# A group's row sums copied ahead of its product with the targets, and waiting for the gathers

## The chip, the cores and the metric

The kernel runs on one core of one Trainium2 chip. The metric is device time of one execution in microseconds (us), the median of three runs. Five engines work side by side, each through its own instruction stream in order: TensorE (PE in the profile, its weight loads PEld), VectorE (DVE), ScalarE (ACT), GpSimd (POOL) and SyncE (SP). They wait for each other through semaphores: an instruction waits until a counter has reached a value, and adds to a counter when it is done. An instruction carries one wait here; further ones stand ahead of it on the same engine as instructions of their own (EVENT_SEMAPHORE in the profile).

## What is computed

For 16,384 users, each with 100 items of history and one target, out of a table of 50,001 items:

```
def _neighbor_attn(E, near_full):
    V = E[near_full]                                  # 32 neighbours of each item
    scores = einsum('nd,nkd->nk', E, V) / sqrt(32)
    return einsum('nk,nkd->nd', softmax(scores), V)
a_sus, a_inf = _neighbor_attn(E_in, near_full), _neighbor_attn(E_out, near_full)
h = concat([E_hist[history], a_sus[history], a_inf[history]])   # 16384 x 100 x 128
t = concat([E_tgt[target],   a_inf[target],  a_sus[target]])    # 16384 x 128
z = relu(einsum('bld,hd->blh', h * t[:, None, :], W1) + b1)     # 128 hidden
scores = einsum('blh,h->bl', z, W2[0])
exp_A = exp(scores) * ((history != target[:, None]) & (history != 0))
attn = exp_A / sum(exp_A, -1)[:, None] ** 0.5
s = sum(h * attn[..., None])                                    # one number
pred = cosine(s * ones, t);   return sigmoid(pred)
```

Of `h * attn` only the sum over everything is wanted, so the kernel needs of each history row its 128 values for the product with the target, and the sum of those values.

## The kernel before, in words

Everything is float32. There are two stages and a short end.

**Stage one** computes the neighbour attention of all items and writes two tables to device memory. `table` holds per item a row of 129 numbers (`W`): first the sum of the item's 128 values, then the values. `ttab` holds the target's values. The change does not touch this stage.

**Stage two** goes through the users in chunks of 128 (`UC` = 128 chunks, one user per partition), and through a chunk's 100 history items in groups of four (`LG`; `NG` = 25 groups a chunk), so through 3200 steps `s`. All engines run it in an order written out by hand. A step issues, in this order:

- `gather(s)`, line 309: four indirect DMAs on POOL (line 316), each of which fetches one row of `table` for each of the 128 users into a buffer `h` of 128 x 4 x 129. There are 20 such buffers (`HBUF`), so the gathers of step s+20 go to the buffer of step s, and wait until all that reads it is done.
- `turn(s)`, line 326: four PE transposes (line 330) turn the 128 values of the four rows into `hT_ps`, one of three PSUM buffers.
- `times_target(s)`, line 332: DVE multiplies `hT_ps` by the chunk's target `tT` into `xT` (line 335, one of six buffers), and then copies the four row sums of `h` to `hsum` (line 338). That copy reads `h` in SBUF itself. It is declared free of a dependency on the four gathers, with the reason that TensorE has read the row: the product before it on DVE waits for the transposes, and these wait for the gathers.
- `hidden(s-3)`, line 345: a PE product with W1 into `z_ps` (line 347), and relu on ACT into `z` (line 349).
- `scored(s-6)`, line 351: a PE product with W2 that adds up in `bank` (line 355).

Once a chunk come the gather of the next chunk's targets (line 280) and `target_work` (lines 288 to 307), and `weights`, `exponents` and `ended`, which turn the chunk's scores into its two sums with `hsum` (lines 359 to 380).

So a buffer `h` has two readers: the transposes on PE and the copy on DVE. The first of the four gathers of step s+20 stands behind a separate wait, for its DMA lane and for DVE's counter, and itself waits for PE's counter.

Of the kernel before, what the change touches and what calls it, by code (L numbers as in the profile page):

```python
# [44 lines left out]
NG = L // LG  # L45
# [8 lines left out]
def kernel(  # L54
# [13 lines left out]
    nc = tc.nc  # L68
# [8 lines left out]
    table = dram.tile([ROWS, W], F32, name="table")  # L77
# [40 lines left out]
    def history_of(i):  # L118
        hists[i] = u_in.tile([P, BSUB, L], I32, name="hidx")
        nc.sync.dma_start(hists[i], hist_v[i])  # L120

    with (
# [23 lines left out]
        def gather(b):  # L146
            v = n_v.tile([P, M, K, 2, G], F32, name="v")
            subs[b]["v"] = v
            for m, s in enumerate(subs[b]["tiles"]):
                it, j = divmod(s, NSUB)  # L150
                if j == NSUB // 2 and it + 1 < NITER:
                    load(it + 1)
                nidx = its[it][0]
                for k in range(K):
                    nc.gpsimd.indirect_dma_start(  # L155
                        out=v[:, m, k].rearrange("p t d -> p (t d)"),
                        out_offset=None,
                        in_=egeo,
                        in_offset=bass.IndirectOffsetOnAxis(ap=nidx[:, j, k : k + 1], axis=0),
                    )  # L160
# [105 lines left out]
    with (  # L266
        tc.manual_schedule(engines={E.PE, E.Activation, E.DVE, E.SP, E.Pool}),
        tc.tile_pool(name="u_x", bufs=6) as u_x,
        tc.tile_pool(name="u_z", bufs=6) as u_z,
        tc.tile_pool(name="u_s", bufs=3) as u_s,  # L270
        tc.tile_pool(name="ps_t", bufs=3, space=bass.MemoryType.PSUM) as ps_t,
        tc.tile_pool(name="ps_z", bufs=3, space=bass.MemoryType.PSUM) as ps_z,
        tc.tile_pool(name="ps_s", bufs=2, space=bass.MemoryType.PSUM) as ps_s,
    ):
        users = {}
        rows, got, hT, xT, z = {}, {}, {}, {}, {}

        def target_rows(c):
            t = u_t.tile([P, D], F32, name="t")
            nc.gpsimd.indirect_dma_start(  # L280
                out=t,
                out_offset=None,
                in_=ttab[0:ITEMS, :],
                in_offset=bass.IndirectOffsetOnAxis(ap=tidx[:, c : c + 1], axis=0),
            )
            users[c] = {"t": t, "hidx": hists[c // BSUB][:, c % BSUB, :]}

        def target_work(c):
            u = users[c]
            t = u["t"]  # L290
            tT_ps = ps_t.tile([P, LG, P], F32, name="hT_ps")
            nc.tensor.transpose(tT_ps[:, 0, :], t, ident)  # L292
            tT = u_t.tile([D, 1, P], F32, name="tT")
            nc.vector.tensor_copy(tT[:, 0, :], tT_ps[:, 0, :])  # L294
            u["tT"] = tT
            nc.vector.tensor_reduce(tsum[:, c : c + 1], t, AX.X, ALU.add)
            junk = u_t.tile([P, D], F32, name="junk")
            nc.scalar.activation(junk, t, AF.Square, accum_out=tsq[:, c : c + 1])
            keep = u_s.tile([P, L], F32, name="keep")
            idf = u_s.tile([P, L], F32, name="idf")  # L300
            nc.vector.tensor_copy(idf, u["hidx"])
            nc.vector.tensor_scalar(keep, idf, 0.0, None, ALU.not_equal)
            nc.vector.scalar_tensor_tensor(  # L303
                keep, idf, tidf[:, c : c + 1], keep, ALU.not_equal, ALU.mult
            )
            u["keep"] = keep
            u["hsum"] = u_s.tile([P, L], F32, name="hsum")

        def gather(s):
            c, g = divmod(s, NG)  # L310
            rows[s] = u_h.tile([P, LG, W], F32, name="h")
            got[s] = []
            for q in range(LG):
                l = g * LG + q
                got[s].append(
                    nc.gpsimd.indirect_dma_start(  # L316
                        out=rows[s][:, q, :],
                        out_offset=None,
                        in_=table,
                        in_offset=bass.IndirectOffsetOnAxis(  # L320
                            ap=users[c]["hidx"][:, l : l + 1], axis=0
                        ),
                    )
                )

        def turn(s):
            c, g = divmod(s, NG)
            hT[s] = ps_t.tile([P, LG, P], F32, name="hT_ps")
            for q in range(LG):
                nc.tensor.transpose(hT[s][:, q, :], rows[s][:, q, 1:W], ident)  # L330

        def times_target(s):
            c, g = divmod(s, NG)
            xT[s] = u_x.tile([D, LG, P], F32, name="xT")
            nc.vector.tensor_tensor(  # L335
                xT[s], hT.pop(s), users[c]["tT"].to_broadcast([D, LG, P]), ALU.mult
            )
            copy = nc.vector.tensor_copy(  # L338
                users[c]["hsum"][:, g * LG : (g + 1) * LG],
                rows.pop(s)[:, :, 0:1].rearrange("p q o -> p (q o)"),  # L340
            )
            for one in got.pop(s):
                tc.declare_no_dep(copy.ins, one.ins, reason="TensorE has read the row")

        def hidden(s):
            z_ps = ps_z.tile([HID, LG, P], F32, name="z_ps")
            nc.tensor.matmul(z_ps, w1T, xT.pop(s), start=True, stop=True)  # L347
            z[s] = u_z.tile([HID, LG, P], F32, name="z")
            nc.scalar.activation(z[s], z_ps, AF.Relu, bias=b1_sb)  # L349

        def scored(s):
            c, g = divmod(s, NG)
            if g == 0:
                users[c]["bank"] = ps_s.tile([NG, LG, P], F32, name="bank")
            nc.tensor.matmul(  # L355
                users[c]["bank"], pick[:, g, :], z.pop(s), start=g == 0, stop=g == NG - 1
            )

        def weights(c):
            flat = u_t.tile([NG, LG, P], F32, name="flat")  # L360
            nc.scalar.copy(flat, users[c].pop("bank"))  # L361
            users[c]["flat"] = flat

        def exponents(c):
            flat = users[c].pop("flat")
            score = ps_t.tile([P, LG, P], F32, name="hT_ps")
            for q in range(LG):
                nc.tensor.transpose(score[:, q, 0:NG], flat[:, q, :], ident[0:NG, 0:NG])  # L368
            users[c]["ea"] = u_s.tile([P, L], F32, name="ea")
            nc.scalar.activation(  # L370
                users[c]["ea"].rearrange("p (g q) -> p q g", q=LG), score[:, :, 0:NG], AF.Exp
            )

        def ended(c):
            u = users.pop(c)
            ea = u["ea"]
            nc.vector.tensor_tensor(ea, ea, u["keep"], ALU.mult)
            nc.vector.tensor_reduce(den[:, c : c + 1], ea, AX.X, ALU.add)
            nc.vector.tensor_tensor(ea, ea, u["hsum"], ALU.mult)
            nc.vector.tensor_reduce(num[:, c : c + 1], ea, AX.X, ALU.add)  # L380

        last = UC * NG
        target_rows(0)
        target_work(0)
        for s in range(last + 2 * LAG + 6):
            c, g = divmod(s, NG)
            if s < last:
                if g == 0 and c % BSUB == 2 and 0 < c // BSUB and c // BSUB + 1 < UC // BSUB:
                    history_of(c // BSUB + 1)
                if g == 5 and c + 1 < UC:  # L390
                    target_rows(c + 1)
                gather(s)
                turn(s)
                times_target(s)
            if 0 <= s - LAG < last:
                hidden(s - LAG)
            if 0 <= s - 2 * LAG < last:
                scored(s - 2 * LAG)
            if s < last and g == 15 and c + 1 < UC:
                target_work(c + 1)  # L400
            done, left = divmod(s - 2 * LAG - NG, NG)
            if 0 <= done < UC and left == 0:
                weights(done)
            if 0 <= done < UC and left == 1:
                exponents(done)
            if 0 <= done < UC and left == 4:
                ended(done)
# [79 lines left out]
```

## Time and profile before

| | us |
|---|---|
| median of 3 runs | 36167.52 |
| lowest, highest | 36134.86, 36170.64 |
| profiled execution | 36233.66 |
| its span, first to last instruction | 36231.5 |

| engine | busy us | share of the span |
|---|---|---|
| PE | 9993.2 | 28% |
| DVE | 6913.8 | 19% |
| ACT | 2690.8 | 7% |
| POOL | 25673.9 | 71% |

A line of the profile names the line of the kernel, the engine, the operation, what it writes and reads, how often, then its busy time in us and the mean of one in ns, and after the bar the idle time of its engine just before it and what ended most of that. PE's ends are modelled. A wait that ends with "issue" has no releaser that the profile shows; "remote" is a semaphore event that it cannot put down to an instruction. A queue with a q behind the engine's name (DVEq, POOLq) is what the engine's instruction stream does by itself, such as separate waits. [...]

### The profile page before, as it was taken

Reading aid. Unit: us, or ns where it says so; the run is one execution under the profiler, and the core shown is the slowest. Engines: PE = TensorE matmul, PEld = TensorE weight load, DVE = VectorE, ACT = ScalarE, POOL = GpSimd, SP = SyncE. Lnnn points to the kernel's source line nnn. Section 1 sums busy time; section 2 is a strip of 40 time slices with the busy share of each in tenths; the row PEclk is TensorE's granted clock in tenths of the full one; section 3 lists DMA queues with packets and bytes.
Section 4 is the critical chain, followed back from the end, with each engine's and each line's share of the span. In section 5 each row is a group of like instructions: output and inputs, shape, how many; then the busy total and the mean of one; then the engine's idle time right before and its main releaser. Section 6 shows DMA issues by size and latency. Waiting matters only on the chain.

```text
span 36231.5 us, 104145 instructions
## 1 busy us (share of the span) xinstructions
PE 9993.2 (28%) x26243; PEld 3238.5 (9%) x26243; DVE 6913.8 (19%) x9965; ACT 2690.8 (7%) x5698; POOL 25673.9 (71%) x25446
## 2 busy tenths in 40 slices
PE   0000000000000000000355555555555555555555
PEld 0000000000000000000111111111111111111111
DVE  2222222222222222222111111111111111111111
ACT  0000000000000000000011111111111111111111
POOL 7777777777777777777666666666666666666666
PEclk9999999999999999999777777777777777777777
DMA  2111111111111111111111111111111111111111
GB/s 46 27 27 27 27 30 27 27 27 27 30 27 27 27 27 27 30 27 25 40 46 46 46 46 46 47 46 47 46 47 47 46 47 46 47 46 46 46 46 44
DMA packets 1027955, 1362.31 MB, mean 38 GB/s; under 512 B 559904, under 2 KB 614432, under 8 KB 1027360
## 3 DMA queue, kind: packets, MB, share of 16 engines
q0 software_dynamic: 814080, 1265.42, 14.5%
q10 hardware_dynamic: 100480, 38.63, 0.6%
q1 hardware_dynamic: 112800, 51.60, 0.6%
q8 instruction: 218, 3.57, 0.0%
q14 instruction: 377, 3.09, 0.0%
HBM read 1315.31 MB, written 51.50 MB: 38 GB/s over the span
## 4 chain that ended last, share of the span: by engine, by line
POOL 37%; another core or an unknown queue 29%; PE 18%; issue 13%; DVE 2%; ACT 1%; DMA 1%; POOLq 0%; ACTq 0%
POOL v L155 37%; PE z_ps L347 7%; PE bank L355 6%; PE hT_ps L330 5%; DVE xT L335 1%; ACT z L349 1%; DMA v<-in_egeo_dram,nidx 1%; DVE hsum L338 0%; PE hT_ps L368 0%; PE hT_ps L292 0%; POOL h L316 0%; ACT flat L361 0%; DVE keep L303 0%; DVE tT L294 0%
## 5 line engine op out<-in xcount | busy, mean ns | idle before, releaser
L316 POOL DMA_INDIRECT h<-table,hidx x12800 | 12078.8, 944 | 6425.1 <-issue 4031.0
L155 POOL DMA_INDIRECT v<-in_egeo_dram,nidx x12512 | 13473.6, 1077 | 4018.1 <-issue 3948.6
L335 DVE TENSOR_TENSOR xT<-hT_ps,tT 128x512 f32<-128x512 f32 x3200 | 2198.3, 690 | 15527.1 <-remote 9754.0
L292 PE MATMUL hT_ps<-ident,t 128*128 128x128 f32 x128 | 45.3, 354 | 17623.6 <-DMA t<-ttab,tidx 17497.8
L347 PE MATMUL z_ps<-xT,w1T 128*128 128x512 f32 x6400 | 4193.1, 743 | 1851.1 <-ACT z L349 1492.8
L330 PE MATMUL hT_ps<-ident,h 128*128 128x128 f32 x12800 | 2538.1, 330 | 5907.6 <-DVE xT L335 4212.6
L355 PE MATMUL bank<-z,pick 128*25 128x512 f32 x6400 | 3982.9, 709 | 0.0
L349 ACT ACTIVATE z<-z_ps,b_sb 128x512 f32<-128x512 f32 x3200 | 2145.0, 686 | 15885.0 <-remote 7292.0
L170 DVE TENSOR_TENSOR prod<-v,own_ps 128x4096 f32<-128x4096 f32 x196 | 864.5, 4411 | 12862.4 <-DMA v<-in_egeo_dram,nidx 12796.7
L330 PEld LDWEIGHTS hT_ps<-ident,h 128*128 128x128 f32 x12800 | 1636.3, 164 | 9061.9 <-DVE xT L335 5285.6
L292 PEld LDWEIGHTS hT_ps<-ident,t 128*128 128x128 f32 x128 | 18.8, 147 | 17756.5 <-issue 17574.9
L187 ACT ACTIVATE ex<-sc,top 128x32 f32<-128x32 f32 x782 | 227.7, 291 | 16707.1 <-DVE top L181 12117.6
L203 DVE TENSOR_TENSOR wv<-v,ex 128x1024 f32<-128x1024 f32 x782 | 1378.3, 1872 | 355.9 <-ACT ex L187 345.0
L347 PEld LDWEIGHTS z_ps<-xT,w1T 128*128 128x128 f32 x6400 | 1179.7, 230 | 2078.2 <-ACT z L349 1680.7
L177 DVE TENSOR_REDUCE sc<-prod 128x128 f32<-128x4096 f32 x196 | 864.5, 4410 | 6.7
L211 DVE TENSOR_REDUCE att<-wv 128x128 f32<-128x4096 f32 x196 | 864.1, 4409 | 6.0
L355 PEld LDWEIGHTS bank<-z,pick 128*25 128x25 f32 x6400 | 434.2, 109 | 3106.7 <-issue 3106.7
L338 DVE COPY hsum<-h 128x4 f32<-128x4 f32 x3200 | 571.1, 178 | 0.0
L368 PE MATMUL hT_ps<-ident,flat 25*128 25x25 f32 x512 | 64.4, 246 | 833.1 <-ACT flat L361 642.0
L280 POOL DMA_INDIRECT t<-ttab,tidx x128 | 120.8, 944 | 55.0 <-issue 50.4
L187 ACT ACTIVATION_READ_ACCUMULATOR ex<-sc,top 128x1 f32 x782 | 146.0, 187 | 0.0
L368 PEld LDWEIGHTS hT_ps<-ident,flat 25*128 25x128 f32 x512 | 50.2, 166 | 966.8 <-ACT flat L361 690.6
(53 smaller groups left out, 849.0 us busy)
## 6 DMA issues: line engine op xcount, KB each, us to landing
h<-table,hidx POOLq DMA_INDIRECT x12800
v<-in_egeo_dram,nidx POOLq DMA_INDIRECT x12512
table<-row ACTq DMA_DIRECT2D x22, 1096.5 KB
own<-in_egeo_dram SPq DMA_DIRECT2D x23, 544.0 KB
row<-in_ehist_dram SPq DMA_DIRECT2D x23, 544.0 KB
ttab<-in_etgt_dram ACTq DMA_DIRECT2D x1, 12500.0 KB
ttab<-row SPq DMA_DIRECT2D x22, 544.0 KB
hidx<-in_history_dram SPq DMA_DIRECT2D x32, 200.0 KB
```

What stands on the lines that cost most here:

```text
L155: nc.gpsimd.indirect_dma_start(out=v[:, m, k].rearrange("p t d -> p (t d)"), out_offset=None, in_=egeo, in_offset=bass.IndirectOffsetOnAxi ...
L170: nc.vector.tensor_tensor(prod[:, 0:n].rearrange("p m k t d -> p m k (t d)"), v.rearrange("p m k t d -> p m k (t d)"), own_ps[:, 0:n].to_b ...
L177: nc.vector.tensor_reduce(sc[:, 0:n].rearrange("p m t k -> p m k t"), prod[:, 0:n], AX.X, ALU.add)
L203: nc.vector.tensor_tensor(wv[:, m, t].rearrange("p d k -> p k d"), subs[b]["v"][:, m, :, t, :], ex[:, m, t, :].rearrange("p (k o) -> p k o ...
L211: nc.vector.tensor_reduce(att[:, 0:n], wv[:, 0:n], AX.X, ALU.add)
L316: nc.gpsimd.indirect_dma_start(out=rows[s][:, q, :], out_offset=None, in_=table, in_offset=bass.IndirectOffsetOnAxis(ap=users[c]["hidx"][: ...
L330: nc.tensor.transpose(hT[s][:, q, :], rows[s][:, q, 1:W], ident)
L335: nc.vector.tensor_tensor(xT[s], hT.pop(s), users[c]["tT"].to_broadcast([D, LG, P]), ALU.mult)
L338: copy = nc.vector.tensor_copy(users[c]["hsum"][:, g * LG : (g + 1) * LG], rows.pop(s)[:, :, 0:1].rearrange("p q o -> p (q o)"),)
L347: nc.tensor.matmul(z_ps, w1T, xT.pop(s), start=True, stop=True)
L349: nc.scalar.activation(z[s], z_ps, AF.Relu, bias=b1_sb)
L355: nc.tensor.matmul(users[c]["bank"], pick[:, g, :], z.pop(s), start=g == 0, stop=g == NG - 1)
```

## The change

The copy of the row sums becomes a function of its own, `sums(s)`, called between `turn(s)` and `times_target(s)`, so on DVE it stands ahead of the product of the same step and behind that of the step before. The declaration is gone: the copy now waits for the four gathers of its step. Nothing else is moved, and no size is changed.

```diff
-        rows, got, hT, xT, z = {}, {}, {}, {}, {}
+        rows, hT, xT, z = {}, {}, {}, {}
...
         def gather(s):
             c, g = divmod(s, NG)
             rows[s] = u_h.tile([P, LG, W], F32, name="h")
-            got[s] = []
             for q in range(LG):
                 l = g * LG + q
-                got[s].append(
-                    nc.gpsimd.indirect_dma_start(
...
+                nc.gpsimd.indirect_dma_start(
...
         def times_target(s):
...
-            copy = nc.vector.tensor_copy(
+
+        def sums(s):
+            c, g = divmod(s, NG)
+            nc.vector.tensor_copy(
                 users[c]["hsum"][:, g * LG : (g + 1) * LG],
                 rows.pop(s)[:, :, 0:1].rearrange("p q o -> p (q o)"),
             )
-            for one in got.pop(s):
-                tc.declare_no_dep(copy.ins, one.ins, reason="TensorE has read the row")
...
                 gather(s)
                 turn(s)
+                sums(s)
                 times_target(s)
```

More of the change, by code (lines that the diff above doesn't have):

```diff
@@ L311, in gather @@
             rows[s] = u_h.tile([P, LG, W], F32, name="h")
-            got[s] = []
             for q in range(LG):
                 l = g * LG + q
-                got[s].append(
[L316 to L323, printed above, removed]
+                nc.gpsimd.indirect_dma_start(
+                    out=rows[s][:, q, :],
+                    out_offset=None,
+                    in_=table,
+                    in_offset=bass.IndirectOffsetOnAxis(
+                        ap=users[c]["hidx"][:, l : l + 1], axis=0
+                    ),
                 )
```

## The prediction

> **What bounds the kernel now.** I read the page first, then the view of the gathers' source line, the table of windows, the timeline, and last the waits that DVE's stream has ahead of its instructions.
>
> ```profile
> span 36231.5 us, 104145 instructions
> PE 9993.2 (28%) x26243; PEld 3238.5 (9%) x26243; DVE 6913.8 (19%) x9965; ACT 2690.8 (7%) x5698; POOL 25673.9 (71%) x25446
> ...
> L316 POOL DMA_INDIRECT h<-table,hidx x12800 | 12078.8, 944 | 6425.1 <-issue 4031.0
> ...
> L280 POOL DMA_INDIRECT t<-ttab,tidx x128 | 120.8, 944 | 55.0 <-issue 50.4
> ```
>
> POOL leads, and no engine is full. From the view of line 316 the first row says when stage two runs, the others what ended POOL's waits and who waited for a gather to land:
>
> ```profile
> L316 POOL DMA_INDIRECT h<-table,hidx x12800: 938/944/1382, 17510.6 to 36171.7; - x197
> L316 POOLq EVENT_SEMAPHORE  x3210: 17/43/19542, 17509.1 to 36161.3; - x189
> ...
>   issue: 4031.0, 11021
>   PE hT_ps L330: 1764.8, 431
> ...
>   PE hT_ps L330: 14.9, 20
> ```
>
> Stage one ends near 17,510.6 us and the change leaves it alone. Stage two's gathers last 36171.7 - 17510.6 = 18,661 us. At an even pace a gather takes 0.944 us and 0.30 us to the next (the "[0.30 <-issue]" of the timeline rows below; 0.302 in the finer times), 1.246 us. The 12,928 of lines 316 and 280 would need 12928 x 1.246 = 16,109 us. The missing 2,552 us are pauses. The last row is the one on landing: PE's transposes waited for a gather 20 times in the whole run, 14.9 us. The rows are there long before they are wanted.
>
> How far ahead POOL runs shows when the two lines are counted in the same windows, gathers first, products second:
>
> ```profile
> 0.00:25020.00 25020.00, 4857.44 (x5147) 0.91 0.15 34
> 0.00:36000.00 36000.00, 11963.65 (x12678) 0.86 0.16 38
> ...
> 0.00:25020.00 25020.00, 870.27 (x1267) 0.91 0.15 34
> 0.00:36000.00 36000.00, 2165.23 (x3152) 0.86 0.16 38
> ```
>
> At 25,020 us 5147 / 4 = 1286.75 groups are issued and 1267 multiplied: 19.75 groups ahead, of 20 buffers. At 36,000 it is 17.5. So POOL is the one that stops, for want of a buffer, and the others are never short of rows. What a pause looks like, in the timeline:
>
> ```profile
> 25014.14 1.12 PE L330 MATMUL hT_ps<-ident,h 128*128 128x128 f32 x4 [7.06 <-DVE xT L335]
> ...
> 25021.21 0.95 POOL L316 DMA_INDIRECT h<-table,hidx  x1 [0.30 <-issue]
> ...
> 25026.05 0.69 DVE L335 TENSOR_TENSOR xT<-hT_ps,tT 128x512 f32<-128x512 f32 x1 [11.89 <-remote]
> 25026.09 1.84 ACT L349 ACTIVATE z<-z_ps,b_sb 128x512 f32<-128x512 f32 x3 [6.41 <-remote]
> 25026.66 0.16 DVE L338 COPY hsum<-h 128x4 f32<-128x4 f32 x1
> 25026.73 0.68 DVE L335 TENSOR_TENSOR xT<-hT_ps,tT 128x512 f32<-128x512 f32 x1
> ...
> 25027.40 0.68 DVE L335 TENSOR_TENSOR xT<-hT_ps,tT 128x512 f32<-128x512 f32 x1
> ...
> 25027.56 0.94 POOL L316 DMA_INDIRECT h<-table,hidx  x1 [5.40 <-PE hT_ps L330]
> ```
>
> The transposes end at 25,015.3 by the model, yet DVE and ACT, which wait for PE's counter, stand until 25,026.05 and are then let go together. By these rows PE's increments come late and in a bunch while the gathers run, and the bunch comes after POOL has stood for some us (its last gather ended at 25,022.16). What holds the increments I cannot see. The end of the pause is plain: the product starts, 0.61 us later the copy, and 25027.56 - 25026.05 = 1.51 us after the product POOL goes on. The first and the last such pause:
>
> ```profile
> 17678.31 0.94 POOL L316 DMA_INDIRECT h<-table,hidx  x1 [0.30 <-issue]
> ...
> 17694.45 0.69 DVE L335 TENSOR_TENSOR xT<-hT_ps,tT 128x512 f32<-128x512 f32 x1 [20.93 <-remote]
> ...
> 17695.96 0.94 POOL L316 DMA_INDIRECT h<-table,hidx  x1 [16.71 <-issue]
> ...
> 36156.46 0.69 DVE L335 TENSOR_TENSOR xT<-hT_ps,tT 128x512 f32<-128x512 f32 x1 [6.30 <-PE z_ps L347]
> 36157.07 0.16 DVE L338 COPY hsum<-h 128x4 f32<-128x4 f32 x1
> ...
> 36157.97 0.94 POOL L316 DMA_INDIRECT h<-table,hidx  x1 [2.38 <-PE hT_ps L330]
> ```
>
> Again 1.51 and 1.51. Counted through the timeline, from the first of these to the last, 530 pauses over 0.6 us end 1.51 us after the product of the step whose buffer is wanted. They last 2,633 us together, 4.97 each, 4.67 beyond the usual 0.30: 530 x 4.67 = 2,475 of the 2,552 us. POOL issues 3200 / 530 = 6.04 groups between two of them. The release of a buffer is the bound of stage two, on top of POOL's pace.
>
> **The change part by part.** *The copy moves.* In the program's order on DVE, the copy of step s now stands behind the product of s-1 and ahead of its own. Nothing it needs is late (20 waits for landing), so it runs as soon as the product of s-1 is out, and when POOL stands for the buffer of s, the copy of s is long done. The separate wait ahead of the gather then costs nothing, and the gather itself waits only for PE's counter, the same increments that let the product start. The 1.51 us from product to POOL fall to between 0 (POOL goes on as the product does) and 0.74 (copy end 36157.23 to POOL 36157.97, what a gather needs behind its separate wait). I take 0.06, near the lower end, because the wait left stands on the gather itself as DVE's does on the product. Gain: 1.45 us a pause, bounds 0.77 and 1.51. Nothing is moved past the gathers on POOL's queue, and SP has no part in it.
>
> *What the shorter pause gives back.* The pause is also what lets PE's increments out, so POOL may be stopped again sooner. Sorted by length, the 530 pauses were followed by these runs: those of 2.06 us (mean of the 105 under 3 us) by 3.1 groups, of 4.21 us (163 from 3 to 5) by 4.9, of 5.62 us (82) by 7.2, of 7.02 us (178 over 6) by 8.1; a straight line through all has 0.95 group for each us. If that holds for the us cut here, a run has 6.04 - 0.95 x 1.45 = 4.66 groups, there are 3200 / 4.66 = 687 pauses of 4.67 - 1.45 = 3.22 us beyond the usual gap, 2,212 us in place of 2,475: 263 us gained. If it does not hold at all, 530 x 1.45 = 769 us are gained, and with the bound 1.51, 800. I take 263, the end that the rows give.
>
> *Waits added on DVE.* The copy has four waits where it had none: two separate ones and one on the copy, 6,400 more separate waits in all. Their price by rows:
>
> ```profile
> L335 DVEq EVENT_SEMAPHORE  x1796: 21/21/21, 17567.1 to 36207.7; - x200
> ...
> L170 DVEq EVENT_SEMAPHORE  x784: 49/50/50, 81.9 to 17494.4; - x196
> ...
> L338 DVE COPY hsum<-h x3200: 150/160/416, 17518.4 to 36210.7; 128x4 f32<-128x4 f32 x189
> ```
>
> Line 170's wait for the gathers of stage one, as these do: 0.05 us each, 0.10 a step, 320 us in all. They lie in DVE's idle time (19% busy; here 11.89 us idle ahead of one product), where behind them wait the copy, the product, and through it PE's next transposes. The cover is gone only in a bunch: the products at 25,026.05, 25,026.73 and 25,027.40 follow each 0.67 us, and the stream may add up to 0.10 us to each. I count 0, since separate waits run ahead in the stream while the engine works; the bound is 320 us, and below zero nothing, for no wait is removed from a product. The wait for the gathers itself is bounded by the 14.9 us above.
>
> [...]
>
> *Sum*, against the profiled execution (span 36,231.5, with 2.2 around it 36,233.7): -263, so 35,970. The median of the runs lies 66 us (0.2%) below the profiled execution, so 36,167.5 - 263 = 35,904.
>
> **The rivals.** *Quiet is what counts.* PE's increments need so much standing of POOL for each group, wherever it is put; then cutting 1.45 us brings pauses in proportion and the total stays 2,475: 36,167. For it: the runs go nearly in proportion to the pauses (1.2 to 1.5 groups per us). Against: the last 1.5 us of a pause come after the bunch is out. About 0.2% is what a measurement of this kernel tells from no change, 72 us.
>
> *The gathers cut the bunch short (slower).* POOL goes on 1.45 us earlier, so its traffic meets the increments that PE makes of the work just let go, and the run gets shorter than the line says. Its place is POOL's first gather after a pause. It decides from the run at which 3.22 us a pause cost what 4.67 did at 6.04 groups: 6.04 x 3.22 / 4.67 = 4.16 groups, against 4.66 forecast. At 3.5 groups: 3200 / 3.5 x 3.22 = 2,944, 469 us more, 36,637; at 3.0, 3,435, or 37,127. For it: the short pauses already have runs of 3.1 groups, near the edge. Against: those 105 cost only 1.76 us beyond the gap, so less per group than the mean. [...] The trace shows late increments, and not by what.
>
> *DVE's added waits come onto the path (slower).* Every product 0.10 us later and PE waiting for each: +320, 36,488. Against it is DVE's 19%.
>
> *The change does not do what it says*: the wait left on the gather could cost the 0.74 us too; with 0.77 gained a pause and the same line the run is 5.31, 603 pauses of 3.90, 2,350: 125 us gained, 36,042, still faster.
>
> **How the numbers follow.** The forecast with its give-back from nothing to the line, and the last rival, 0.50: faster, 35,367 (gain 800) to 36,042; its own likeliest value is 35,904. Quiet counts: 0.17, same. Bunch cut short: 0.22; waits on the path: 0.11; slower, 0.33 together. The range goes from 35,350 to 36,650, the cut bunch at 3.5 groups; some 0.12 lie above it and 0.05 below.
>
> **What would show it.** In the profile after: the copy of a step ahead of its product and separate waits of line 338 near 0.05 us (right if DVE's waits are hidden); in each pause POOL's gather within 0.1 us of the product of 20 steps before, instead of 1.51; gathers still 15 to 20 groups ahead; line 316's idle near 6,425 - 263 = 6,160 us; 600 to 700 pauses of about 3.5 us. It is wrong if the idle before line 316 grows, if pauses pass 770 (a run under 4.16), or if products start late with PE's counter already there.

## The result, and the profile after

| | before | after |
|---|---|---|
| median of six runs, us | 36,160.1 | 35,910.85 |
| lowest, highest | 36,134.86, 36,174.48 | 35,906.39, 35,917.14 |
| profiled execution | 36,233.66 | 35,906.39 |

The ratio is 0.9932, 95% interval 0.992 to 0.9945: 249 us less by the medians. The profiled executions lie 327 us apart, because that of before was 74 us above its own median.

One thing is needed to read the rest. The runs fell on different chips, and the same kernel does not take the same time on all of them: the kernel before took 36,160 us here, 36,254 us on the chip of the last experiment, and 31,810 to 31,824 us on those of the others. Every comparison below is made on one chip.

The page after, and the view of the gathers' line (314 now, 316 before); the columns are those of the rows shown of before:

```profile
span 35904.2 us, 110545 instructions
PE 10007.5 (28%) x26243; PEld 3232.4 (9%) x26243; DVE 6900.4 (19%) x9965; ACT 2672.6 (7%) x5698; POOL 25676.7 (72%) x25446
...
L314 POOL DMA_INDIRECT h<-table,hidx x12800 | 12080.2, 944 | 6091.9 <-issue 3281.1
...
L338 DVE COPY hsum<-h 128x4 f32<-128x4 f32 x3200 | 558.5, 175 | 18.6 <-DMA h<-table,hidx 17.6
```

```profile
L314 POOL DMA_INDIRECT h<-table,hidx x12800: 938/944/1795, 17507.1 to 35836.6; - x197
L314 POOLq EVENT_SEMAPHORE  x3210: 17/43/13331, 17505.7 to 35825.3; - x189
```

POOL is as busy as before and a gather takes the same 944 ns. What shrank is the idle time ahead of the gathers, 6,425.1 to 6,091.9 us, that is 333 us. Stage one still ends at 17,507; stage two's gathers last 35836.6 - 17507.1 = 18,329.5 us in place of 18,661.1: 331.6 less, all of the gain. The 6,400 more instructions (110,545 against 104,145) are the separate waits of the copy:

```profile
L338 DVEq EVENT_SEMAPHORE  x6400: 21/35/50, 17512.7 to 35880.5; - x194
L338 DVE COPY hsum<-h x3200: 155/160/418, 17513.9 to 35881.0; 128x4 f32<-128x4 f32 x189
its engine sat idle before it (us, times) until:
  DMA h<-table,hidx: 17.6, 5
```

The waits take 21 to 50 ns, and the copy waited for a row to land five times, 17.6 us in all. The timeline shows a pause; first the one near the time shown of before, then the first of stage two:

```profile
25061.46 0.94 POOL L314 DMA_INDIRECT h<-table,hidx  x1 [0.30 <-issue]
25067.61 0.69 DVE L332 TENSOR_TENSOR xT<-hT_ps,tT 128x512 f32<-128x512 f32 x1 [15.20 <-remote]
25067.65 1.84 ACT L347 ACTIVATE z<-z_ps,b_sb 128x512 f32<-128x512 f32 x3 [9.16 <-remote]
25067.85 0.94 POOL L314 DMA_INDIRECT h<-table,hidx  x1 [5.44 <-remote]
25068.22 0.16 DVE L338 COPY hsum<-h 128x4 f32<-128x4 f32 x1
25068.29 0.68 DVE L332 TENSOR_TENSOR xT<-hT_ps,tT 128x512 f32<-128x512 f32 x1
...
25068.89 0.16 DVE L338 COPY hsum<-h 128x4 f32<-128x4 f32 x1
25068.96 0.68 DVE L332 TENSOR_TENSOR xT<-hT_ps,tT 128x512 f32<-128x512 f32 x1
```

```profile
17669.19 0.69 DVE L332 TENSOR_TENSOR xT<-hT_ps,tT 128x512 f32<-128x512 f32 x1 [20.93 <-remote]
17669.42 0.94 POOL L314 DMA_INDIRECT h<-table,hidx  x1 [6.86 <-remote]
```

The product and POOL are now let go by the same event: POOL follows the product by 0.24 us (25067.85 - 25067.61, 17669.42 - 17669.19), where it was 1.51. The copy behind the product already belongs to the next step. In the bunch the products still follow each other 0.67 to 0.68 us apart (25,067.61, 25,068.29, 25,068.96), with a copy and its waits between them.

Counted through the whole timeline of the two profiled executions, in the way the 530 pauses were counted:

| pauses that end a fixed time after the product | before | after |
|---|---|---|
| number | 530 | 663 |
| groups from one to the next | 6.04 | 4.83 |
| from the product to POOL, us each | 1.51 | 0.235 |
| mean length, us | 4.97 | 3.45 |
| standing ahead of the product, all, us | 530 x 3.46 = 1,834 | 663 x 3.215 = 2,132 |
| from the product to POOL, all, us | 530 x 1.51 = 800 | 663 x 0.235 = 156 |

So the tail of the pauses lost 644 us, and 298 of these came back as standing ahead of the product, in 133 more pauses. That is what "gives back" meant in the prediction, now as two rows. The count, here and in the prediction, goes from one gather of history rows to the next, so a gather of the next chunk's targets (line 280) that stands between two of them counts as 1.25 us of pause. With that gather taken as work there are 528 such pauses of 4.93 us before and 661 of 3.41 after, and the standing ahead of the product goes from 1,808 to 2,099 us, so the reading stays the same.

### The profile page after: what moved, and what is told of

Read it like the earlier page. It is cut to its first block, busy times and chain, and to the rows that moved or that the text cites. A ratio compares the mean times of both kernels' runs of the same rounds, so it can differ in the third digit from the quotient of the medians.

```text
span 35904.2 us, 110545 instructions
## 1 busy us (share of the span) xinstructions
PE 10007.5 (28%) x26243; PEld 3232.4 (9%) x26243; DVE 6900.4 (19%) x9965; ACT 2672.6 (7%) x5698; POOL 25676.7 (72%) x25446
## 4 chain that ended last, share of the span: by engine, by line
POOL 38%; another core or an unknown queue 22%; PE 19%; issue 19%; ACT 1%; DVE 1%; DMA 1%; DVEq 0%; POOLq 0%; ACTq 0%
POOL v L155 37%; PE z_ps L345 7%; PE bank L353 7%; PE hT_ps L327 5%; ACT z L347 1%; POOL h L314 1%; DMA v<-in_egeo_dram,nidx 1%; DVE xT L332 1%; DVE hsum L338 0%; DMA h<-table,hidx 0%; PE hT_ps L366 0%; PE hT_ps L292 0%; ACT flat L359 0%; DVEq L338 0%
## 5 line engine op out<-in xcount | busy, mean ns | idle before, releaser
L314 POOL DMA_INDIRECT h<-table,hidx x12800 | 12080.2, 944 | 6091.9 <-issue 3281.1
L155 POOL DMA_INDIRECT v<-in_egeo_dram,nidx x12512 | 13475.0, 1077 | 4013.3 <-issue 3950.2
L338 DVE COPY hsum<-h 128x4 f32<-128x4 f32 x3200 | 558.5, 175 | 18.6 <-DMA h<-table,hidx 17.6
```

Of the source, the lines that this page charges most:

```text
L155: nc.gpsimd.indirect_dma_start(out=v[:, m, k].rearrange("p t d -> p (t d)"), out_offset=None, in_=egeo, in_offset=bass.IndirectOffsetOnAxi ...
L314: nc.gpsimd.indirect_dma_start(out=rows[s][:, q, :], out_offset=None, in_=table, in_offset=bass.IndirectOffsetOnAxis(ap=users[c]["hidx"][: ...
L338: nc.vector.tensor_copy(users[c]["hsum"][:, g * LG : (g + 1) * LG], rows.pop(s)[:, :, 0:1].rearrange("p q o -> p (q o)"),)
```

## The experiments

Two theories were tested. **Release:** the time from the product to POOL falls, because the copy no longer stands in the release of the buffer; the added waits cost nothing; and part of the gain is given back, because PE's increments are late. **Waits:** the change of the declaration and the waits that come with it cost or bring something by themselves.

**The waits without the move.** The copy stays behind the product, and only the declaration goes:

```diff
-            copy = nc.vector.tensor_copy(
+            nc.vector.tensor_copy(
...
-            for one in got.pop(s):
-                tc.declare_no_dep(copy.ins, one.ins, reason="TensorE has read the row")
```

> The order of before (copy behind its product), but the copy's waits for its four gathers are kept: the change's waits without its move. Theory A (the gain comes from the release of the buffer, which no longer runs through product and copy): 36,160 us within 72, pauses end 1.51 us after the product as before, DVE's 6,400 separate waits are hidden. Rival B (the added waits cost something on DVE): slower, up to 320 us, 36,480. Rival C (the waits themselves make the gain, by pacing DVE): near 35,911.

Measured 31,823.95 against 31,824.28 for before on the same chip, ratio 1.0 (0.9991 to 1.0009). Repeated on a second chip of that kind:

> The order of before with the copy's waits for its gathers kept (20 buffers), once more, in case the kernel before takes 36,160 us here and not 31,810. Theory A: 36,160 within 72 in that case, with pauses that end 1.51 us after the product; rival C (the waits make the gain): 35,911; rival B (the waits cost): up to 36,480. Where the kernel before takes 31,810 us all three say the same, 31,810.

31,813.79 against 31,812.43, ratio 1.0 (0.9991 to 1.001). The waits are hidden in both. But the gain could not be seen on these chips, as the run of the changed kernel itself shows further on.

**No copy at all** (the changed kernel without the copy; `hsum` is set to 1, so the row sums are left out of the result):

```diff
+            nc.vector.memset(u["hsum"], 1.0)
...
-            nc.vector.tensor_copy(
-                users[c]["hsum"][:, g * LG : (g + 1) * LG],
-                rows.pop(s)[:, :, 0:1].rearrange("p q o -> p (q o)"),
-            )
+            rows.pop(s)
```

> The changed kernel without the copy of the row sums and its waits (hsum is set to one once a chunk, so the sums are left out of the result). The buffer is then read by PE alone. Theory A: same as the changed kernel, 35,911 within 72, pauses end about 0.235 us after the product. Rival B: the waits and the copy cost something in the changed kernel, so up to 320 us less than it, 35,590. Rival C: without waits the gain is gone, 36,160.

**Eight buffers** in the changed kernel (`HBUF = 8`):

> The changed kernel with 8 buffers of gathered rows in place of 20. Theory A (a pause lets PE's increments out, whatever the depth at which POOL is stopped): within 150 us of 35,911, gathers 4 to 8 groups ahead of the products. Rival D (the depth hides late increments; a product waits up to 31.5 us, six groups of 5 us, so 8 are too few): slower by several hundred us, more than 36,160.

31,822.18 (ratio 0.9999, 0.999 to 1.0008) and 31,823.61 (1.0, 0.9991 to 1.0009): nothing, both against 31,824.28. On this chip neither the copy nor twelve buffers matter.

**No gathers** (only the first 20 steps fetch rows; all later steps compute on those):

```diff
+            if s >= HBUF:
+                rows[s] = kept[s % HBUF]
+                return
+            rows[s] = kept[s] = hold.tile([P, LG, W], F32, name=f"h{s}")
```

> The changed kernel with gathers in the first 20 steps of stage two alone; later steps reuse their rows (all other gathers of history rows are left out). Theory A (PE's increments come late while gathers run): products start within 0.1 us of the transposes' end, and stage two goes at PE's pace, 2.4 us a group at the full clock to 4.9 at half: 7.7 to 15.7 ms, 25,300 to 33,200 us in all. Rival E (PE's increments are late by themselves): waits of many us ahead of the products remain, and the time is 33,000 us or more.

One execution took 23,526.44 us. Its page and the view of its gathers' line:

```profile
span 23524.7 us, 85220 instructions
...
L335 DVE TENSOR_TENSOR xT<-hT_ps,tT 128x512 f32<-128x512 f32 x3200 | 2211.6, 691 | 4867.7 <-PE hT_ps L330 4867.1
```

```profile
L317 POOL DMA_INDIRECT h<-table,hidx x80: 940/944/985, 15649.4 to 15749.7; - x80
```

Stage two lasted (23,524.7 - 15,649) / 3200 = 2.46 us a group without gathers, against 4 x 1.246 = 4.98 us that POOL needs for four. The granted clock was 1.00 in this stage, and 0.81 in the changed kernel's own run on this chip; at 0.81 an estimate from the two, 2.46 / 0.81 = 3.0 us, is still below 4.98. So the gathers are stage two's bound on this chip. Stage two's 7,876 us lie in the 7,700 to 15,700 that were expected for it; the sum of 25,300 and more was missed because it took stage one at 17,510 us, and here it takes 15,649. What makes PE's increments late it could not tell, because here they are not late with the gathers either.

**The changed kernel on such a chip:**

> The changed kernel itself, beside the kernel before on the same chip. Theory A (the change only shortens pauses in which POOL stands for a buffer): where the trace shows no such pauses and POOL is one group ahead, as in the first set of runs at 31,824 us, same within 0.1%; where the kernel before takes 36,160 us, ratio 0.993 again. Rival C (the move or the waits help DVE or PE themselves): faster by some 0.7% on either.

31,807.3 against 31,810.08, ratio 0.9999 (0.999 to 1.0008): no gain. Its page and the view of the gathers' line say why:

```profile
span 31804.7 us, 110545 instructions
...
L314 POOL DMA_INDIRECT h<-table,hidx x12800 | 12078.0, 944 | 3901.2 <-issue 3563.5
...
L332 DVE TENSOR_TENSOR xT<-hT_ps,tT 128x512 f32<-128x512 f32 x3200 | 2211.4, 691 | 520.5 <-PE hT_ps L327 327.7
```

```profile
L314 POOLq EVENT_SEMAPHORE  x3210: 17/43/43, 15640.8 to 31767.6; - x189
...
  DVE hsum L338: 12307.2, 3148
```

A separate wait of POOL never took over 43 ns, so POOL never stood for a buffer. The idle time of 3,901.2 us over 12,800 gathers is the usual 0.30 each. No product waits for "remote", and the gathers last 31,779 - 15,642 = 16,137 us, POOL's own pace. The last row shows who waits instead: the copy, now ahead of its product, for rows to land, 3,148 times. By the same view a gather lands 2.5 us after it starts (median). The copy's wait brought no loss, and PE stands for the same rows: its transposes 4,181 us, until they land. Where POOL did not stand for a buffer, the faster release brought nothing.

**One buffer.** To have the release on the path on a chip where PE's increments are not late, before, after and the waits alone were run with `HBUF = 1`: every group then waits for the release of the last.

> The kernel before with 1 buffer of gathered rows in place of 20, so that POOL stands for the buffer in every group and the release is in the path 3200 times. Theory A: a group takes 3 x 1.246 us to the last gather, 2.5 to its landing, 0.5 of transposes and 1.51 from product to POOL: 8.3 us, 26,500 us in stage two, 42,200 in all where stage one takes 15,650. POOL goes on 1.51 us after each product.

> The changed kernel with 1 buffer in place of 20. Theory A: POOL goes on 0.24 us after each product, or where the copy's own end plus 0.74 is later, 0.45: 1.06 to 1.27 us less a group than the kernel before with one buffer, 3,400 to 4,060 us less in all. Rival C (the release is not what the change moves): the two with one buffer within 300 us of each other.

> The order of before with the copy's waits for its gathers kept, with 1 buffer. Theory A: as the kernel before with one buffer within 100 us, since the waits are over when the copy's turn comes. Rival B (the two separate waits delay the copy, and so the buffer): 0.05 to 0.10 us a group later, 160 to 320 us more. Rival C (the waits make the gain): as the changed kernel with one buffer.

One execution each: 42,624.47 before, 39,299.68 after, 42,617.33 with the waits alone. The move brings 3,325 us, 1.04 us a group; the waits alone change 7 us. In the timeline, before and then after:

```profile
30006.36 0.69 DVE L335 TENSOR_TENSOR xT<-hT_ps,tT 128x512 f32<-128x512 f32 x1 [7.55 <-PE hT_ps L330]
30006.97 0.16 DVE L338 COPY hsum<-h 128x4 f32<-128x4 f32 x1
30007.87 0.95 POOL L316 DMA_INDIRECT h<-table,hidx  x1 [2.38 <-DVE hsum L338]
```

```profile
30007.66 0.17 DVE L338 COPY hsum<-h 128x4 f32<-128x4 f32 x1 [6.28 <-DMA h<-table,hidx]
...
30008.03 0.69 DVE L332 TENSOR_TENSOR xT<-hT_ps,tT 128x512 f32<-128x512 f32 x1 [0.20 <-PE hT_ps L327]
30008.57 0.94 POOL L314 DMA_INDIRECT h<-table,hidx  x1 [2.71 <-PE hT_ps L327]
```

Before: 30007.87 - 30006.36 = 1.51, the same number as with 20 buffers. After: 30008.57 - 30008.03 = 0.54 here, 0.476 in the median, and not 0.235. With one buffer the copy is as late as the transposes, and POOL still follows the end of the copy by 30008.57 - 30007.83 = 0.74 us. That is why 3,325 came and not the 3,400 and more expected. The waits of POOL say the same in sums, before, after, and with the waits alone:

```profile
POOL h L316 <- DVE hsum L338: 10920.3, 3012, 4.4
```

```profile
POOL h L314 <- PE hT_ps L327: 7836.4, 3033, 3.6
```

```profile
POOL h L316 <- DVE hsum L338: 10924.4, 3012, 4.5
```

**Pauses made by hand.** Every tenth step PE was given 18 products more, so that POOL would stand for a buffer also where increments are not late: with three buffers before and after, and with 20 after.

```diff
+        def held():
+            z_ps = ps_z.tile([HID, LG, P], F32, name="z_ps")
+            full = pick.rearrange("p a b -> p (a b)")[:, 0 : LG * P]
+            for _ in range(18):
+                nc.tensor.matmul(
+                    z_ps.rearrange("p a b -> p (a b)"), ident, full, start=True, stop=True
+                )
...
+                if s % 10 == 5:
+                    held()
```

> The kernel before with 3 buffers in place of 20, and with 18 extra PE products of 128x512 into a spare z_ps buffer ahead of the transposes of every tenth step (nobody reads them): a hold of PE that does not depend on the gathers, 15 to 20 us, 320 times, long enough to stop POOL for want of a buffer. Theory A: about one pause a hold, each ended 1.51 us after the product of the step whose buffer is wanted; with pauses of 5 to 10 us, 33,400 to 35,000 us in all.

> The changed kernel with the same 3 buffers and the same 320 holds. Theory A: pauses end about 0.24 us after the product, 1.27 us earlier, and here, where the hold does not depend on POOL's standing, nothing is given back: 320 x 1.27 = 406 us less than the kernel before with them, within 80. If a shorter pause is given back anyway (runs get shorter, more pauses): 100 to 200 us less. Rival C (the release is not what the change moves): the same.

> The changed kernel with its 20 buffers and the 320 holds of PE. Theory A: 20 buffers are 100 us of gathers, more than a hold, so POOL never stands and the time is that without holds, 31,810 within 0.3%. Rival F (a hold of PE stops POOL even with 20 buffers, as in the first profile): over 32,500.

These fell on the chip where the kernel before takes 36,254.29, so the absolute figures expected, which were worked out for 31,810, are missed. Measured: 37,222.23 (ratio 1.0269, 1.0251 to 1.0286), 36,961.85 (1.0194, 1.0177 to 1.0211) and 36,406.01 (1.004, 1.0025 to 1.0054). After is 260 us below before at three buffers. That lies between the two amounts expected, 326 to 486 if nothing is given back and 100 to 200 if it is. A pause of each in the timeline:

```profile
24998.97 0.69 DVE L335 TENSOR_TENSOR xT<-hT_ps,tT 128x512 f32<-128x512 f32 x1 [17.94 <-PE hT_ps L330]
24999.58 0.16 DVE L338 COPY hsum<-h 128x4 f32<-128x4 f32 x1
25000.48 0.94 POOL L316 DMA_INDIRECT h<-table,hidx  x1 [7.08 <-PE z_ps L355]
```

```profile
25015.68 0.69 DVE L332 TENSOR_TENSOR xT<-hT_ps,tT 128x512 f32<-128x512 f32 x1 [12.48 <-remote]
25015.92 0.95 POOL L314 DMA_INDIRECT h<-table,hidx  x1 [4.62 <-remote]
```

Again 1.51 and 0.24. Before had 696 such pauses and after 670, so the tail alone fell from 696 x 1.51 = 1,051 to 670 x 0.235 = 157 us. Of these 894 us, 260 reached the time: 71% was given back. With 20 buffers the kernel after paid an estimated 36,406 - 36,254 x 0.9932 = 398 us for 320 holds, and 556 less than with three. So the expectation that with 20 buffers the holds cost nothing was missed too: 398 us are 1.1%, where 0.3% was allowed. That is a look at the buffers rather than at the change.

The move with 20 buffers was thus only run where increments are late, and the waits alone only where they are not. At 20 buffers the split between the two rests on the one-buffer runs.

## Why the prediction was right

*The bound.* Right. All of the gain lies ahead of line 316's (now 314's) gathers, and where POOL never stands for a buffer the same change gives 0.9999.

*The copy moves.* Right in kind, a little large in size: 0.235 us from product to POOL, where 0.06 was taken, so 1.27 us a pause instead of 1.45, inside the bounds 0.77 and 1.51. The rival that the wait left would cost 0.74 too falls by the same rows. The runs show both prices side by side. From the end of a copy that a separate wait stands for, POOL needs 0.74 us; from the event that a wait on the gather itself stands for, it is 0.235 behind DVE. The records of POOL's stream go with the two numbers. In the pauses of after, the stream's next separate wait begins 0.22 us before the held gather starts (median), so the stream had already left that gather behind; before, the gather starts 0.70 us after its separate wait has ended (median). What the stream does in those 0.70 us no run shows. The 0.235 is also outside the 0.1 us that the prediction set as the sign.

*What the shorter pause gives back.* Right in amount, and this is the step that carried the number; the reason given with it was only half right. The line put through 1.27 gives 6.04 - 0.95 x 1.27 = 4.83 groups a run, and 3200 / 663 = 4.83 were measured. Had nothing been given back, 530 x 1.27 = 673 us would have been gained; it was 249 by the medians. The pauses were 3.45 - 0.30 = 3.15 us beyond the gap, where 3.22 was forecast with 687 of them: 2,088 us against 2,212. That is 124 us more gained than the sum said, on pauses of this kind. The other pauses, those not ending with a product, went from 208 to 263 us beyond the gap and took 55 of it back (much of both figures is the targets' gathers; with those taken as work it is 94 and 152).

Against the rival "quiet is what counts" the prediction held that "the last 1.5 us of a pause come after the bunch is out". The recorded increments of PE's counter say otherwise. Take the pauses that have a bunch of eight increments or more. Before, the bunch holds 15 (median) and ends 1.00 us before POOL goes on. After, it holds 11 and ends 0.08 us behind the start of POOL's gather; with three buffers and the holds described above it is 15 and 11 again. So POOL, going on earlier, meets the bunch, and less of it is let out. The runs of groups behind these pauses fell from 8.6 to 7.8, those behind the other pauses from 3.5 to 2.1. In both traces a run goes with the number of increments recorded in its pause (correlation 0.86 and 0.87) more than with the pause's length (0.58 and 0.62). A straight line through the lengths stood in for that, and that it came out at 4.83 to the second digit is partly luck. No run changed the size of a bunch and nothing else, so that the shorter bunch is what gives the gain back is argued from these records, which have gaps (last section), and not shown.

*Waits added on DVE.* Right: counted at nothing. They take 21 to 50 ns each, a median of 35, and in the trace of after 6,388 of the 6,400 begin while DVE is still at an earlier instruction, so they ran ahead of the work, as the prediction counted on, rather than in idle time. With the waits alone the ratio was 1.0 twice, and 7 us in 42,624 with one buffer.

*The sum.* 35,904 forecast, 35,910.85 measured. Part of that closeness is chance. The wake came out 0.175 us longer than taken, and the standing ahead of the product, which the sum left at 4.97 - 1.51 = 3.46 us a pause, came out at 3.215. Between the profiled executions 327 us are missing, 64 more than forecast; but by the medians it is 249, because the profiled execution of before was an unusually long one, 74 us above its median. So the pauses that the two traces show differ by more than the kernels do.

*The rivals.* "Quiet is what counts" asked for the same total of pauses, and the ratio's interval ends at 0.9945. But a part of it is in the rows: standing ahead of the product grew from 1,834 to 2,132 us. "The gathers cut the bunch short" was to decide under 4.16 groups a run; 4.83 were seen. With three buffers and holds, where it had most room, after was still 260 us faster. So it did not make the kernel slower, but by the records of PE's counter what it describes took place: the bunch went from 15 increments to 11. "DVE's added waits" fell with the waits run alone, and with the products of a bunch, which follow each other no more slowly than before.

*The reason given for late increments* is not shown. The prediction said that they come late "while the gathers run". On the other chips the same gathers run, 944 ns each and 1.25 us apart, and no product waits for "remote". So running gathers alone do not hold PE's increments. What does stays open: no kernel here told it apart, because none of them brought the lateness to a chip that did not have it, or took it from one that did.

## What to carry to other kernels

A buffer that is read by two engines is released by the later of them (here POOL went on 1.51 us after the product with the copy last, 0.235 with it first): put the short reader where it never ends the release, ahead of the long work of its own engine, even if it then needs waits of its own. The price is read at the waiting engine, from the event that lets both go to the instruction that was held. Before counting that price times the number of pauses, sort the pauses by length and see what run of work follows each: here a straight line through that told within 4% how many pauses there would be (687 against 663), and half of the gain or more was gone by it. Look also at what the waiting engine's return does to the others: here, by the records, it cut short what the pause had just let go, from 15 increments to 11. And ask first whether the engine stands for that buffer at all: on the chip where POOL did not, the same change gave 0.9999.

## What was not expected of the hardware

- The same program took 31,810 us on some chips and 36,160 to 36,254 on others. Both stages differ. In the changed kernel's two pages, the gathers of stage one, which the change does not touch, take 1,077 ns on the first chip and 943 on the second; DVE stands 15,155 us ahead of its products on the first, 8,982 of them ended by "remote". On the second it stands 520.5 there, and 12,307 ahead of the copy, for rows to land:

```profile
L155 POOL DMA_INDIRECT v<-in_egeo_dram,nidx x12512 | 13475.0, 1077 | 4013.3 <-issue 3950.2
...
L332 DVE TENSOR_TENSOR xT<-hT_ps,tT 128x512 f32<-128x512 f32 x3200 | 2197.1, 690 | 15155.0 <-remote 8981.8
```

```profile
L155 POOL DMA_INDIRECT v<-in_egeo_dram,nidx x12512 | 11804.1, 943 | 3819.1 <-issue 3771.8
```

- Where PE's increments are late, they come in steps of about 0.70 us, and after POOL has stood, 14 to 18 of them 34 to 43 ns apart (10 to 13 after the change). In the trace of before, all 266 bunches of eight or more came while POOL stood, and none while it ran. What holds them is open. These traces do not hold every semaphore event: of PE's 19,331 increments the trace of before has 15,701, and of DVE's 9,070 it has 5,522. So a wait ended by "remote" may be one whose event was lost. That the engines stand is shown by their own instructions all the same: the product at 25,026.05 started 29 us after its own transposes had ended (at 24,997.03 by the model; the transposes at 25,014.14, which the prediction sets beside it, belong to the product two steps on).
- A gather held by a separate wait starts 0.74 us after the end of the copy that it waits for, one held by its own wait 0.235 us after DVE's start on the same event. The two are counted from different marks.
